# Perceiver decoder on one Trainium2 core: the block FFN computed on its chosen tokens, with rows gathered and weights addressed by register

## The chip, the cores and the metric

The program runs on one NeuronCore of a Trainium2 chip. A core has five engines with instruction queues of their own: TensorE (PE; its weight loads are listed as PEld), VectorE (DVE), ScalarE (ACT), GpSimd (POOL) and SyncE (SP), which here only issues transfers. Sixteen DMA engines move data between HBM and the on-chip memory SBUF; PE writes its results to PSUM, from where DVE or ACT copies them. The metric is the device time of one execution in microseconds (us), lower is better. All data are fp32.

## The reference

```python
x = x + L0_xattn(layernorm(x), ctx)     # 16 heads, 1024 queries in 16 sequences, 1601 keys
x = x + L0_mamba(layernorm(x))
x = x + L0_ffn(layernorm(x))            # the stage that is changed
x = x + L1_xattn(layernorm(x), ctx)     # the stage after it
x = x + L1_attn(layernorm(x))
x = x + L1_ffn(layernorm(x))

def L0_ffn(x):                          # n = 1024 tokens, IN_F 512, OUT_F 2048, 16 blocks of 128
    prob = softmax(xf @ router_w.T + router_b)
    _, idx = top_k(prob, 4)
    mask = zeros((n, 16), bool).at[arange(n)[:, None], idx].set(True)
    h = einsum('nd,ibd->nib', xf, w1b) + b1b
    h = relu(where(mask[:, :, None], h, 0))
    return einsum('nib,dib->nd', where(mask[:, :, None], h, 0), w2b) + b2
```

Each of the 1024 tokens uses 4 of the 16 blocks. Ties in the router's logits go to the lower block number.

## The kernel before

The 1024 tokens are kept as `x`, eight tiles of 128 rows by 512 (`G = 8`), normalised and transposed into `xnT` (512 features on 4 times 128 partitions, 1024 tokens along a row). The six sub-layers are stages that follow each other. A tile framework places the instructions and their semaphores; what is wrapped in `pin(...)`, or issued by `pmm`, keeps the order of the program on its engine, the rest is placed by the framework's scheduler. Every engine works its queue in order.

*The scan stage* (`st2`) ends with a loop over g = 0 to 7: `decay`, `mixing`, `gated` and `mixed` for tile g, and normalisation and transposition of tile g - 2. The last two tiles are normalised behind it, the very last one (`ln_out(G - 1, ps3)`) inside the FFN.

*The block FFN* (`st3`, L720 to L915) computes all 16 blocks for all tokens and zeroes what was not chosen. For each half q of 512 tokens, `for i in range(NBLK)` forms block i's 128 hidden units in four products of 512 columns (PE), applies bias and ReLU (ACT, L857) and multiplies by the block's mask (DVE, `masked`, L840). Then `down` forms the second product, 16 blocks into each of four row tiles, and the result is added to `x` (L900, L908).

The masks come from `route(q)` (L749 to L783): router products on PE, the rank of each logit among the 16 by comparing all pairs (four DVE passes over 1024 elements and a reduction), and `rank < 3.5`. The mask is transposed on PE, stored to HBM (`kept`, L781) and read back broadcast over all partitions, two blocks at a time (`load_mask`, L789).

Between the products of the two halves other work is placed: `fold_weights` (the next attention's query and key weights multiplied into one matrix `W`, and its bias row `wb`), `bias_part`, six pieces of the last FFN's weights that are still to be quantised (`piece_load` to `piece_turn`, with stores L187), and `ln_out` of tiles that are ready. When the second half's first products are done, the space of `w1` is released and the first context tiles for the next stage are loaded (`load_T(0)`, `load_N(0)`).

*The second cross attention* (`st4`) needs, for each tile of 128 queries, the projected queries `qtT` (`folded_q`, 512 tokens at a time), scores against 1601 keys of two sequences (`scores4`), a maximum (DVE, L965), exponentials (ACT), transposes (`transpose4`), the weighted sum (`attend4`) and an output product (`output4`). Its loop over g issues `scores4(g + 1)` ahead of the work of tile g. The context is loaded one or two tiles ahead on SP's queue.

The other stages are not touched.

Of the kernel before, what the change touches and what calls it, by code (L numbers as in the profile page):

```python
# [9 lines left out]
F32 = mybir.dt.float32  # L10
AF = mybir.ActivationFunctionType
ALU = mybir.AluOpType
# [3 lines left out]
P = 128  # L16
# [17 lines left out]
QMAX = 32767.0  # L34

# [12 lines left out]
def perceiver_kernel(ctx: ExitStack, tc: tile.TileContext, x_d, ctxT_d, ctx_d, cols_d, rows_d,  # L48
# [9 lines left out]
    def mm(out, lhsT, rhs, start=True, stop=True):  # L58
        pe.matmul(out, lhsT=lhsT, rhs=rhs, start=start, stop=stop)  # L59

# [79 lines left out]
    def add_rows(bias, g0=0, g1=G):  # L140

        for g in range(g0, g1):
# [8 lines left out]
              for n, shape in (("wgt", [D, FI]), ("wut", [D, FI]), ("wdt", [FI, D]))]  # L151
    pieces = ([(wgate_d[f * P:(f + 1) * P, :], turned[0][:, f * P:(f + 1) * P])
# [41 lines left out]
    with ExitStack() as st1:  # L194
# [19 lines left out]
        pin = tc.keep_in_program_order  # L214

        def pmm(out, lhsT, rhs, start=True, stop=True):
            pin(pe.matmul(out, lhsT=lhsT, rhs=rhs, start=start, stop=stop))  # L217

# [312 lines left out]

    with ExitStack() as st2:
# [142 lines left out]
        for g in range(G):  # L675
            if g == 4:
                make_bc(1)
            pd = decay(g)
            if g == 1:
                new = mixing(g, pd)  # L680
            if g:
                gated(g - 1, mt)
            if g >= 2:
                ln_scale(g - 2, g - 1, pin)
                xn = ln_norm(g - 2)
            mt = new if g == 1 else mixing(g, pd)
            if g:
                mixed(g - 1)
            if g >= 2:
                ln_transpose(g - 2, xn, ps2)  # L690
# [3 lines left out]
        ln_scale(G - 2, G - 1)  # L694
        ln_out(G - 2, ps2)
        ln_scale(G - 1, G)

    cT, cN, ctxt, ctxn = {}, {}, {}, {}

    def load_T(g):  # L700

        for b in (2 * g, 2 * g + 1) if g < G else ():
            cT[b] = ctxt[g % 2].tile([P, 2, LK], F32, name="cT", tag="cT")
            pin(nc.sync.dma_start(out=cT[b], in_=ctxT_d[b].rearrange("(c p) k -> p c k", p=P)))

    def load_N(g):

        for b in (2 * g, 2 * g + 1) if g < G else ():
            cN[b] = ctxn[g % 2].tile([P, KC, CD], F32, name="cN", tag="cN")
# [4 lines left out]

    with ExitStack() as st3:
# [3 lines left out]
        w2, hT = [], []  # L721
        for i in range(4):
            w2.append(big.tile([P, 4, D], F32, name="w2", tag=f"w2{i}"))
            hT.append(big.tile([P, 4, 512], F32, name="hT", tag=f"hT{i}"))
            nc.sync.dma_start(out=w2[i], in_=w2_d[:, 4 * i * D:4 * (i + 1) * D].rearrange(
                "p (i e) -> p i e", i=4))
        wq1 = load_w("wq1", wq1_d).rearrange("p (c e) -> p c e", c=4)
        wkv1 = load_w("wkv1", wkv1_d)


        bias = const.tile([P, 3], F32, name="bias", tag="bias")
        sums = const.tile([P, G + 1], F32, name="sums", tag="sums")
        wb = row(R_BV0)

        kept = dram.tile([NBLK, NT], F32, name="kept", tag="kept")
        st3a = st3.enter_context(ExitStack())
        mkp = pool(st3a, "mkp", bufs=3)
        masks = {}
        tmp = pool(st3a, "tmp3", bufs=2)
        psr = pool(st3, "psr", bufs=2, space=PSUM)  # L740
        ps3 = pool(st3, "ps3", bufs=6, space=PSUM)
        prep = pool(st3a, "prep", bufs=2)
        todo = list(range(NPREP, 3 * FC))

        lg = tmp.tile([P, G, NBLK], F32, name="lg", tag="lg", bufs=1)
        def route(q):  # L749


            pr = psr.tile([P, 512], F32, name="pr", tag="pr")
            for c in range(4):
                mm(pr[32 * c:32 * c + 32, :], rwz[:, c, :], xnT[:, c, q * 512:(q + 1) * 512])
            lp = tmp.tile([P, 512], F32, name="lp", tag="xn")
            s.copy(lp, pr)
            yield
            pr = psr.tile([P, 4, NBLK], F32, name="pl", tag="pr")
            for k in range(4):
                mm(pr[:, k, :], lp[:, k * P:(k + 1) * P], four[:, :NBLK])  # L760
            v.tensor_tensor(lg[:, 4 * q:4 * q + 4, :], pr,
                            row(R_RB, NBLK).unsqueeze(1).to_broadcast([P, 4, NBLK]), ALU.add)
            l4 = lg[:, 4 * q:4 * q + 4, :]
            shape = [P, 4, NBLK, NBLK]
            li = l4.unsqueeze(3).to_broadcast(shape)
            lj = l4.unsqueeze(2).to_broadcast(shape)
            gt = tmp.tile(shape, F32, name="gt", tag="gt", bufs=1)
            eq = tmp.tile(shape, F32, name="eq", tag="eq", bufs=1)
            v.tensor_tensor(gt, lj, li, ALU.is_gt)
            v.tensor_tensor(eq, lj, li, ALU.is_equal)  # L770
            v.tensor_tensor(eq, eq, before.unsqueeze(1).to_broadcast(shape), ALU.mult)
            v.tensor_tensor(gt, gt, eq, ALU.add)
            rank = tmp.tile([P, 4, NBLK], F32, name="rank", tag="rank", bufs=1)
            v.tensor_reduce(rank, gt, AX.X, ALU.add)
            v.tensor_scalar(rank, rank, TOPK - 0.5, None, ALU.is_lt)
            pr = psr.tile([NBLK, 4, P], F32, name="pt", tag="pr")
            for i in range(4):
                pe.transpose(pr[:, i, :], rank[:, i, :], ident)
            keepT = tmp.tile([NBLK, 512], F32, name="keepT", tag="keepT", bufs=1)
            s.copy(keepT, pr.rearrange("p a b -> p (a b)"))  # L780
            nc.sync.dma_start(out=kept[:, q * 512:(q + 1) * 512],  # L781
                              in_=keepT)
            yield  # L783

        def load_mask(n):
            q, i = divmod(n, NBLK)
            if q < 2:
                masks[n] = mkp.tile([P, 2, 512], F32, name="mk", tag="mk")
                nc.sync.dma_start(  # L789
                    out=masks[n],  # L790
                    in_=kept[i:i + 2, q * 512:(q + 1) * 512].partition_broadcast(P))

        wkT = wkv1[:, 0:1024].rearrange("p (c e) -> p c e", c=4)
        wv1 = wkv1[:, 1024:2048].rearrange("p (c e) -> p c e", c=2)
        W = wq1[:, :, 0:CD]

        def fold_weights():


            wqT = [tmp.tile([P, 2, D], F32, name="wqT", tag=n, bufs=1) for n in ("gt", "eq")]  # L800
# [4 lines left out]
            for e in range(4):  # L805
                ps = ps3.tile([P, 4, P], F32, name="ps", tag="mm")
                for c in range(4):
                    pe.transpose(ps[:, c, :], wq1[:, c, e * P:(e + 1) * P], ident)
                evac(part(e), ps.rearrange("p c d -> p (c d)"))
            ps = ps3.tile([P, D], F32, name="ps", tag="mm")  # L810
            for e in range(4):
                mm(ps, col(C_BK1 + e).to_broadcast([P, P]), part(e), e == 0, e == 3)
            s.copy(wb, ps)
            v.tensor_reduce(sums[:, G:], wb, AX.X, ALU.add)
            for h in range(2):
                ps = ps3.tile([P, 2, CD], F32, name="ps", tag="mm")
                for i in range(2):
                    c = 2 * h + i
                    for e in range(4):
                        mm(ps[:, i, :], part(e)[:, c * P:(c + 1) * P], wkT[:, e, :],  # L820
                           e == 0, e == 3)
                evac(W[:, 2 * h:2 * h + 2, :], ps)

        def bias_part(i):
            if i == 0:
                pbs.append(ps3.tile([P, 3], F32, name="pb", tag="mm"))
            for e in range(4):
                mm(pbs[0][:, i:i + 1],
                   wkT[:, e, i * P:(i + 1) * P] if i < 2
                   else col(C_BK1 + e).to_broadcast([P, P]), col(C_BQ1 + e), e == 0, e == 3)  # L830
            if i == 2:
                v.tensor_copy(bias, pbs[0])

        pbs = []
        routes = [route(q) for q in range(2)]
        next(routes[0])

        def masked(q, i):
            h = hT[i // 4][:, i % 4, :]
            v.tensor_tensor(h, h, masks[16 * q + i - i % 2][:, i % 2, :], ALU.mult)  # L840
            if i % 2:
                load_mask(16 * q + i + 5)

        def bias_product(g, pin=free):

            xw = lnp.tile([P, D], F32, name="xw", tag="xn")
            gp.tensor_tensor(xw, x[:, g, :], wb, ALU.mult)
            pin(v.tensor_reduce(sums[:, g:g + 1], xw, AX.X, ALU.add))

        for q in range(2):  # L850
            t = slice(q * 512, (q + 1) * 512)
            for i in range(NBLK):
                ps = ps3.tile([P, 512], F32, name="ps", tag="mm")
# [554 lines left out]
```

## Time and profile before

| what | value |
|---|---|
| median of 3 runs | 1940.64 us (1936.29 to 1941.37) |
| the profiled execution | 1943.53 us; its span, first to last instruction, 1941.8 us |
| mean granted clock of PE | 0.987 of full speed |
| PE, start of the FFN's first product | 1214.8 us after the span's start |
| PE, start of the second cross attention | 1456.7 us |
| PE, start of the third layer (L1 self attention) | 1600.2 us |
| tile loop of the attention, one tile of queries | 15.2 us (weighted sums start at 1486.05, 1501.21, 1516.37) |
| moved to and from HBM | 127.02 MB read, 11.60 MB written |

How to read the profile: a row of a group gives line, engine, operation, the program's names of result and operands, shapes and count, then the busy time in us, the mean of one in ns, and the idle time of the engine just before with what ended it. A matmul in fp32 appears as two passes. The ends of matmuls are modelled, so single matmuls overlap a little; the distance between starts is their pace. Times in a timeline are us from the start of the span.

### The profile page before, as it was taken

What the parts mean: (1) busy time and instruction counts of PE and PEld (TensorE: products, weight loads), DVE (VectorE), ACT (ScalarE), POOL (GpSimd) and SP (SyncE); (2) the same over time, 40 slices, a digit from 0 to 9 for tenths busy, and PEclk for the clock granted to TensorE, in tenths of its full rate; (3) what the DMA queues carried; (4) which work ended last, traced back from release to release, by engine and by line L of the source; (5) the groups of instructions that cost most, each with busy time, mean ns of one, the idle gap of its engine ahead of it and who ended that gap; (6) DMA issues with size and microseconds to landing.
All of it is one profiled execution on the core that took longest, in us unless ns stands there. A gap on an engine that the chain in (4) does not pass through costs nothing.

```text
span 1941.8 us, 41193 instructions
## 1 busy us (share of the span) xinstructions
PE 1885.0 (97%) x18111; PEld 1056.6 (54%) x18111; DVE 1047.0 (54%) x1622; ACT 790.9 (41%) x1521; POOL 651.7 (34%) x589
## 2 busy tenths in 40 slices
PE   8999999999999999999999899999999999999599
PEld 4566666666666666666666554445444554444244
DVE  4566666666666666666666455622103335229641
ACT  3355455455555554555555356201103232226700
POOL 0365556555555565554555332111002000000200
PEclk9999999999999999999999999999999999999899
DMA  6012021201120121112020211620256971010001
GB/s 220 1 47 58 12 57 47 56 14 51 53 55 15 47 57 23 47 46 58 14 56 7 88 78 34 207 55 12 80 199 261 409 284 51 0 49 17 0 0 44
DMA packets 110084, 141.28 MB, mean 73 GB/s; under 512 B 79520, under 2 KB 82096, under 8 KB 106320
## 3 DMA queue, kind: packets, MB, share of 16 engines
q1 hardware_dynamic: 109904, 138.64, 21.7%
q8 instruction: 142, 2.33, 0.5%
q14 instruction: 38, 0.31, 0.1%
HBM read 127.02 MB, written 11.60 MB: 71 GB/s over the span
## 4 chain that ended last, share of the span: by engine, by line
PE 93%; DVE 3%; issue 2%; ACT 1%; DMA 1%; POOL 0%; SPq 0%; ACTq 0%; POOLq 0%; DVEq 0%
PE ps L217 42%; PE ps L59 24%; PE sc L217 10%; PE av L217 6%; PE po L59 4%; PE u L217 2%; PE ps L133 1%; PE pbc L59 1%; DVE sc L268 1%; PE pd L59 1%; POOL gate L1285 0%; PE busy L217 0%; PE pg L59 0%; ACT at L988 0%; DVE st L116 0%
## 5 line engine op out<-in xcount | busy, mean ns | idle before, releaser
L217 PE MATMUL ps<-wkv,ctxT 128*128 128x256 f32 (+1 forms) x1664 | 412.7, 383 | 0.0
L217 PE MATMUL ps<-ctxT,wkv 128*128 128x400 f32 (+1 forms) x1024 | 408.1, 521 | 0.8 <-DMA ctxT<-in_ctxT_dram 0.8
L217 PEld LDWEIGHTS ps<-wkv,ctxT 128*128 128x128 f32 (+1 forms) x1664 | 304.0, 186 | 116.3 <-ACT kt L233 5.6
L268 DVE TENSOR_REDUCE sc<-sc 128x4 f32<-128x1664 f32 x128 | 243.0, 1898 | 197.6 <-PE sc L217 197.6
L304 POOL TENSOR_TENSOR acc<-acc,st 128x512 f32<-128x512 f32 x252 | 320.5, 1272 | 19.8
L295 DVE STREAM_TRANSPOSE st<-et 128x832 f32<-128x832 f32 x256 | 264.9, 1035 | 57.8 <-ACT et L286 51.7
L233 ACT ACTIVATE kt<-ps,cols 128x400 f32<-128x400 f32 (+1 forms) x256 | 155.1, 606 | 323.9 <-PE ps L217 323.9
L286 ACT ACTIVATE et<-sc,nm 128x416 f32<-128x416 f32 x512 | 269.6, 610 | 33.4 <-DVE nm L280 33.3
L217 PEld LDWEIGHTS ps<-ctxT,wkv 128*128 128x128 f32 x1024 | 174.5, 190 | 162.8 <-issue 81.9
L251 ACT COPY vt<-ps 128x256 f32<-128x256 f32 (+1 forms) x288 | 107.2, 372 | 180.2 <-PE ps L217 177.1
L302 POOL TENSOR_TENSOR acc<-st 128x512 f32<-128x512 f32 x63 | 80.2, 1273 | 199.3 <-DVE st L295 141.3
L217 PE MATMUL sc<-kt,xnT 32*32 32x416 f32 x4096 | 126.8, 523 | 3.6 <-ACT et L286 2.8
L59 PE MATMUL ps<-xnT,w 128*128 128x512 f32 x256 | 112.7, 594 | 0.0
L217 PE MATMUL av<-st,vt 128*32 128x64 f32 x6656 | 106.9, 220 | 3.7 <-issue 2.8
L59 PE MATMUL ps<-w,hT 128*128 128x512 f32 x256 | 110.2, 592 | 0.0
L217 PEld LDWEIGHTS av<-st,vt 128*32 128x32 f32 x6656 | 96.3, 110 | 25.4 <-issue 24.3
L175 POOL TENSOR_TENSOR w<-w,winv 128x512 f32<-128x512 f32 x36 | 37.7, 1049 | 194.1 <-DVE winv L171 192.3
L1285 POOL TENSOR_TENSOR gate<-up,gate 128x1024 f32<-128x1024 f32 x5 | 11.8, 2358 | 250.3 <-ACT up L1284 250.3
L180 POOL TENSOR_TENSOR w<-w,wsc 128x512 f32<-128x512 f32 x36 | 38.5, 1070 | 137.1 <-DVE w L179 137.1
L59 PE MATMUL ps<-xnT,wuT 128*128 128x512 f32 x192 | 82.8, 592 | 0.0
L59 PEld LDWEIGHTS ps<-w,hT 128*128 128x128 f32 x256 | 48.6, 190 | 61.2 <-issue 61.2
L59 PEld LDWEIGHTS ps<-xnT,w 128*128 128x128 f32 x256 | 47.6, 190 | 56.3 <-issue 56.2
(248 smaller groups left out, 2092.9 us busy)
## 6 DMA issues: line engine op xcount, KB each, us to landing
cT<-in_ctxT_dram SPq DMA_DIRECT2D x16, 1601.0 KB, 9.7
cN<-in_ctx_dram SPq DMA_DIRECT2D x16, 1536.0 KB, 11.1
ctxT<-in_ctxT_dram SPq DMA_DIRECT2D x15, 1601.0 KB, 6.5
mk<-kept SPq DMA_DIRECT2D x16, 512.0 KB, 4.1
w<-in_w_dram SPq DMA_DIRECT2D x1, 4096.0 KB, 13.5
w<-in_w_dram SPq DMA_DIRECT2D x4, 1024.0 KB, 6.9
w<-in_wgate_dram SPq DMA_DIRECT2D x12, 256.0 KB, 4.3
wgt<-room SPq DMA_DIRECT2D x48, 64.0 KB, 2.5
```

The source lines that it names most:

```text
L59: pe.matmul(out, lhsT=lhsT, rhs=rhs, start=start, stop=stop)
L133: pin(pe.transpose(ps[:, c, :], xn[:, c * P:(c + 1) * P], ident))
L175: pin(gp.tensor_tensor(w, w, inv.unsqueeze(2).to_broadcast([P, 16, 32]), ALU.mult))
L180: pin(gp.tensor_tensor(w, w, sc.unsqueeze(2).to_broadcast([P, 16, 32]), ALU.mult))
L217: pin(pe.matmul(out, lhsT=lhsT, rhs=rhs, start=start, stop=stop))
L233: pin(s.activation(kt[:, o:o + n], ps[:, :n], AF.Identity, bias=col(C_BK0 + c)))
L251: pin(s.copy(t[:n, :], ps[:n, :]))
L268: pin(v.tensor_reduce(top, sc[:, :, 0:KW], AX.X, ALU.max))
L286: pin(s.activation(ets[u, g][:, r, :], qks[u, g][0][:, r, 0:KW], AF.Exp, bias=nms[u, g][:, r:r + 1]))
L295: pin(v.transpose(tts[u, i][:, h, r].rearrange("p r k q -> p (r k q)"), ets[u, g][:, r, :].rearrange("p r c -> p (r c)")))
L302: pin(gp.tensor_tensor(acc, t[:, :, 0:2], t[:, :, 2:4], ALU.add))
L304: pin(gp.tensor_tensor(acc, acc, t[:, :, k:k + 2], ALU.add))
```

## The change

After the change the FFN is computed for the chosen pairs of token and block only. Each normalised tile is stored to HBM by rows (`xn_d`). The router's first half runs in the last iteration of the scan's loop, its second half behind it. From the ranks the kernel works out, for each token's four blocks, a place in a list sorted by block in which every block's part is filled up to whole tiles of 128: 47 tiles in any case. `places` counts with triangular and all-ones products on PE; one-hot tiles (written into `xnT`, which is free now) and the 32 columns `where` are multiplied on PE to give `listed`, the token number of each place. `block` holds each tile's block times 128, `btab` its bias, and `slots` the place of each token's four results.

A loop over the 47 tiles then fetches 128 rows by an indirect DMA on POOL's queue, transposes them on PE, multiplies them by their block's part of `w1` and, transposed again, of `w2`, both addressed by a register that PE loads from `block` four tiles at a time, and stores 128 rows of results to HBM (`y_d`). In the attention stage `arrive(g)` fetches four result rows for each token of tile g, again by indirect DMA, and adds them to `x`. The queries are then projected by tile (`prepare`) and not by half; the first tiles ahead of the loop, tile g + 2 inside iteration g. The masks, their store and their loads are gone. The folding of the attention's weights stands ahead of the tile loop, the six remaining weight pieces partly ahead of it and partly in it.

The diff, cut to its core:

```diff
+TILES = (NT * TOPK - P) // P + NBLK
+    xn_d = dram.tile([NT, D], F32, name="xnd", tag="xnd")
+    y_d = dram.tile([TILES * P, D], F32, name="yd", tag="yd")
...
+    def keep_rows(g, xn):
+        pin(nc.sync.dma_start(out=xn_d[g * P:(g + 1) * P, :], in_=xn))
+    def logits(q, psum, lp, lg):
+        pr = psum()
+        for c in range(4):
+            pmm(pr[32 * c:32 * c + 32, :], rwz[:, c, :], xnT[:, c, q * 512:(q + 1) * 512])
+        s.copy(lp, pr)
...
+        for k in range(4):
+            pmm(pl[:, k, :], lp[:, k * P:(k + 1) * P], four[:, :NBLK])
+        v.tensor_tensor(lg, pl, row(R_RB, NBLK).unsqueeze(1).to_broadcast([P, 4, NBLK]), ALU.add)
+    def compare(lg, gt, eq, on):
...
+        v.tensor_tensor(gt, lj, li, ALU.is_gt)
+        v.tensor_tensor(eq, lj, li, ALU.is_equal)
+        on.tensor_tensor(eq, eq, before.unsqueeze(1).to_broadcast(shape), ALU.mult)
+        on.tensor_tensor(gt, gt, eq, ALU.add)
+    def ranks(q, gt):
+        v.tensor_reduce(rk[:, t], gt, AX.X, ALU.add)
+        v.tensor_scalar(kept[:, t], rk[:, t], TOPK - 0.5, None, ALU.is_lt)
...
+        for g in range(4 * q, 4 * q + 4):
+            v.tensor_tensor(seen[:, g + 1], seen[:, g], kept[:, g], ALU.add)
+        for k in range(TOPK):
+            v.tensor_scalar(pick[:, t, k], rk[:, t], float(k), None, ALU.is_equal)
...
             pd = decay(g)
+            if g == G - 1:
...
+                for _ in logits(0, ...): pass
+                compare(lg, gt, eq, gp)
...
             if g >= 2:
+                keep_rows(g - 2, xn)
                 ln_transpose(g - 2, xn, ps2)
...
-        w2, hT = [], []
-        def route(q): ...
-        def load_mask(n): ...
-        def masked(q, i): ...
-        for q in range(2): ...
+            def places(q, on):
+                pmm(at, ahead, kept[:, 4 * q:4 * q + 4].rearrange("p g e -> p (g e)"), True, False)
+                pmm(at, ones, seen[:, 4 * q:4 * q + 4].rearrange("p g e -> p (g e)"), False, True)
...
+                for n in range(16 * q, 16 * q + 16):
+                    g, k = divmod(n, TOPK)
+                    on(n).tensor_scalar(xnT[:, k, g * P:(g + 1) * P], iota, lane[:, n:n + 1],
+                                        None, ALU.is_equal)
...
+            compare(lg, gt, eq, v)
+            places(0, lambda n: gp)
+            fold_bias()
+            bias_parts()
+            ranks(1, gt)
+            places(1, lambda n: gp if n % 4 == 3 else v)
...
+            for n in range(4 * G):
+                v.tensor_scalar(where[:, n, :], iota[:, :TILES], tileof[:, n:n + 1],
+                                ids[:, n // 4:n // 4 + 1], ALU.is_equal, ALU.mult)
+            fold_half(0)
+            for n in range(4 * G):
+                g, k = divmod(n, TOPK)
+                pmm(pw, xnT[:, k, g * P:(g + 1) * P], where[:, n, :], n == 0, n == 4 * G - 1)
+            pin(v.tensor_copy(listed, pw))
...
+        def gather(t):
+            pin(gp.indirect_dma_start(
+                out=rooms[:, t % 5, :], out_offset=None, in_=xn_d,
+                in_offset=bass.IndirectOffsetOnAxis(ap=listed[:, t:t + 1], axis=0)))
+        def turn_in(t):
+            for c in range(4):
+                pin(pe.transpose(ps[:, c, :], rooms[:, t % 5, c * P:(c + 1) * P], ident))
+            s.copy(rooms[:, 5 + t % 3, :], ps.rearrange("p c k -> p (c k)"))
+        def up_product(t):
+            if t % 4 == 0:
...
+                ins, vals = nc.values_load_multi_w_load_instructions(
+                    block[0:1, t:t + n], engines=[mybir.EngineType.PE], ...)
...
+            for c in range(4):
+                pmm(ps, rooms[:, 5 + t % 3, c * P:(c + 1) * P],
+                    w1[:, c, bass.ds(picks[t], P)], c == 0, c == 3)
+            v.tensor_copy(hs[t], ps)
+        def turn_h(t):
+            pin(pe.transpose(ps, hs.pop(t), ident))
+            s.activation(hTs[t], ps, AF.Relu, bias=btab[:, t:t + 1])
+        def down_product(t):
+            pmm(ps, hTs.pop(t), w2[:, bass.ds(picks.pop(t) * 4, D)])
+            v.tensor_copy(y, ps)
+            nc.sync.dma_start(out=y_d[t * P:(t + 1) * P, :], in_=y)
+        for t in range(5):
+            gather(t)
+        for t in range(TILES + 3):
+            if t < TILES:
+                turn_in(t)
+                if t + 5 < TILES:
+                    gather(t + 5)
+            if 0 <= t - 1 < TILES:
+                up_product(t - 1)
+            if 0 <= t - 2 < TILES:
+                turn_h(t - 2)
+            if t >= 3:
+                down_product(t - 3)
+            if t == 2:
+                load_T(0)
+            if t == 8:
+                load_N(0)
+            if t < G:
+                pin(gp.tensor_tensor(x[:, t, :], x[:, t, :], row(R_B2), ALU.add))
...
+        def arrive(g):
+            for k in range(TOPK):
+                n = TOPK * g + k
+                pin(gp.indirect_dma_start(
+                    out=ys[:, k, :], out_offset=None, in_=y_d,
+                    in_offset=bass.IndirectOffsetOnAxis(ap=slots[:, n:n + 1], axis=0)))
+            for k in range(TOPK):
+                pin(v.tensor_tensor(x[:, g, :], x[:, g, :], ys[:, k, :], ALU.add))
+            ln_stats(g, pin)
...
-        def folded_q(h): ...
-        def q_bk(h): ...
+        def prepare(g):
+            ln_transpose(g, ln_norm(g, pin), ps_mm, pin)
+            for c2 in range(2):
+                for c in range(4):
+                    pmm(ps, W[:, c, c2 * P:(c2 + 1) * P], xnT[:, c, t], c == 0, c == 3)
+                pin(s.activation(qtT[:, c2, t], ps, AF.Identity, bias=bias[:, c2:c2 + 1]))
+            pin(v.tensor_tensor(xw, x[:, g, :], wb, ALU.mult))
+            pin(v.tensor_reduce(sums[:, g:g + 1], xw, AX.X, ALU.add))
...
+        arrive(0)
+        ln_scale(0, 1, pin)
+        prepare(0)
+        scores4(0)
+        load_T(2)
+        arrive(1)
+        arrive(2)
+        ln_scale(1, 3, pin)
+        prepare(1)
         for g in range(G):
             if g + 1 < G:
                 scores4(g + 1)
...
+            if g == 0:
+                arrive(3)
+                arrive(4)
+            if g == 1:
+                for k in range(5, G):
+                    arrive(k)
+                ln_scale(3, G, pin)
...
             transpose4(g)
+            if g + 2 < G:
+                prepare(g + 2)
             if g:
                 output4(g - 1)
             attend4(g)
```

## Prediction

> **What bounds the kernel now.** I read the page's busy times first, then the chain of waits, then busy times by stage, then the timelines around the two ends of the block FFN, and last the transfers.
>
> The page: TensorE (PE) is the bound, and the FFN's two products are two of its costly groups.
>
> ```profile
> PE 1885.0 (97%) x18111; PEld 1056.6 (54%) x18111; DVE 1047.0 (54%) x1622; ACT 790.9 (41%) x1521; POOL 651.7 (34%) x589
> L59 PE MATMUL ps<-xnT,w 128*128 128x512 f32 x256 | 112.7, 594 | 0.0
> L59 PE MATMUL ps<-w,hT 128*128 128x512 f32 x256 | 110.2, 592 | 0.0
> ```
>
> The columns are count, busy us, mean ns, idle. 128 products stand as 256 passes, so an fp32 product of 512 columns takes two passes of 0.44 us. Together 222.9 us, which the change attacks.
>
> Busy times in three stretches (FFN, second cross attention, the rest) and in one short one near the end:
>
> ```profile
> 1215.00:1457.00 242.00, 242.00 (x654) 113.79 (x653) 63.81 (x108) 30.09 (x48) 25.38 (x21) 1.00 0.33 111
> 1457.00:1600.00 143.00, 140.52 (x900) 74.35 (x899) 47.09 (x104) 45.67 (x93) 10.80 (x13) 1.00 0.82 319
> 1600.00:1942.00 342.00, 310.14 (x755) 139.24 (x753) 163.63 (x265) 110.91 (x156) 11.79 (x5) 0.95 0.07 25
> ...
> 1846.00:1852.00 6.00, 5.37 (x8) 2.17 (x9) 5.51 (x7) 0.23 (x1) 0.58 (x1) 0.52 0.00 0
> ```
>
> After the length come PE, weight loads, DVE, ACT, POOL, granted clock, DMA share, GB/s. In the FFN PE never rests: routing, masks and folding are hidden. In the attention PE rests 2.5 us.
>
> The timeline of PE, with durations that I use below:
>
> ```profile
> 1214.35 0.60 PE L133 MATMUL ps<-ident,xn 128*128 128x128 f32 x4
> 1606.99 1.16 PE L59 MATMUL sc<-KT,QT 64*128 64x128 f32 x8
> 1846.63 5.35 PE L217 MATMUL busy<-gate,ident 128*128 128x512 f32 x6 [22.41 <-DVE gate L1291]
> 1851.93 2.74 PE L217 MATMUL busy<-wdT,ident 128*128 128x512 f32 x6
> ```
>
> Four transposes take 0.60, eight 128-column passes 1.16. Six passes after a rest of 22.41 us took 2.6 us longer than six later ones: the clock of 0.52 above.
>
> Transfers (KB each, median us from issue to landing):
>
> ```profile
> w<-in_wup_dram SPq DMA_DIRECT2D x12, 256.0 KB, 3.8
> w<-in_wgate_dram SPq DMA_DIRECT2D x12, 256.0 KB, 4.3
> out_dram<-ot SPq DMA_DIRECT2D x8, 256.0 KB, 2.0
> ```
>
> A gathered tile, 128 rows of 2 KB, has 256 KB too.
>
> **The sum's start.** The profiled execution took 1943.5 us, span 1941.8 and 1.7 around it, 2.9 above the median of 1940.6. PE starts the FFN at 1214.8, the attention at 1456.7 (241.9 later) and the third layer at 1600.2 (143.5 later). What follows is unchanged.
>
> **Step 1: the last scan iteration, +2.7.** The first half's router now stands in it. PE's passes there only move (they were in the FFN), but DVE gets 0.23 + 1.23 + 1.22 (logits, two comparisons) ahead of the product that PE waits for. POOL's two comparison passes are under PE's work.
>
> **Step 2: the list, which nothing covers.** The FFN's first product needed one transposed tile; the first gather needs the whole list. From the last output product's end, 1214.5 + 2.7 = 1217.2: add, statistics, root, reciprocal, normalisation 0.63 + 0.68 + 0.17 + 0.29 + 0.12 + 0.65 = 2.5, and in DVE's queue between them two roundings and a transpose of weight pieces (0.89 + 0.89 + 0.67): 1222.2. Transposes, copy, router passes, copy, logit passes 0.60 + 0.59 + 1.06 + 0.57 + 0.96, and 1.0 for five hand-overs (some 0.2 each): 1227.0. Logits 0.23, four comparisons 4.9, reduction 1.2, kept 0.2, four picks (0.2) and four running sums (0.15) 1.4, the first half's places 1.2: 1236.1. Then PE's small products 0.5, eight-odd DVE passes of 256 or 512 elements 2.7 (0.35 and 0.67, by 1.22 for 1024), seven small ones 1.1, twelve one-hot tiles 2.4 (0.2 each, by 0.43 for 512), 32 columns of the list 5.4 (0.17 each, by the 0.16 of the smallest rows), a reduction 0.69, the copy 0.16: list at 1249.1. One gather 4.0 (between 3.8 and 4.3): first tile at 1253.1, 38.3 after the FFN's start. The folding of the attention's weights (some 16 us of PE) fits under this wait.
>
> **Step 3: the tile loop.** 47 tiles of 128 rows always, whatever is chosen. PE per tile: four transposes 0.60, eight passes of 128 columns 1.16, one transpose 0.15, two passes of 512 0.86: 2.77. Beside it per tile DVE 0.9, ACT 0.9, POOL one issue: all covered. No row shows a product with a register address (five per tile, a register instruction ahead of each). From below 0; from above 0.35 each, what SP's queue takes to issue a transfer; I take 0.08, twice the 38 ns of a queue's semaphore instruction, its nearest kin: 3.17 per tile. Twelve register loads: 0.04 to 1.6 (the 32 KB store of the mask landed in 1.6); I take 0.4. So 149 + 5 + 4 for draining three tiles. Gathers are five tiles ahead (16 us) and land in 4.3: covered. Row stores stand in SP's queue behind context loads that land in 9.7 and 11.1, but three buffers and two PSUM banks are 16 us: covered; were the cover gone, some 5 us each. Loop's end 1411, 45.7 earlier than now.
>
> **Step 4: rows back, T = 1411.** 32 more gathers, into one set of four buffers, and DVE takes them in program order behind each score maximum. I price POOL's issue at 1.0 (its nearest row, 1.05 for a 512-column pass; bounds 0.35 from SP's issue and 2.36, its longest pass) and 3.0 more to land (2.0 to 4.3), so four gathers take 7.0. Copy 0.69, issue and store 2.3: T+3.0. Row set 0 landed T+10.0, last add and statistics T+11.6, root and normalisation T+12.8, transposes, copy, 16 passes, bias T+17.0, scores 5.5 and maximum 2.2 T+24.7. Set 1 is there: four adds and statistics 3.7, T+28.4. Set 2's issue starts when set 1's first buffer is read, T+25.4: landed T+32.4, normalised T+35.2, projected T+39.4, scores and maximum T+47.1. Set 3 T+50.8; set 4 issued T+47.8, landed T+54.8; tile 2 projected T+60.8. Behind this projection in PE's queue stands the first weighted sum: it starts at T+60.8, where it now starts 29.4 after the stage's start. Then sum and scores 11.2, maximum 2.2, set 5 T+77.9, set 6 landed T+81.9, set 7 T+86.6, tile 3 projected T+93.2; the second weighted sum starts at T+94.1, now at 44.5: +49.6. Four later tiles are projected one by one inside the loop: transposes 0.6, 16 passes 2.3, a wait for ACT's copy 0.9, four times: +15.2. Loads, masks and POOL's adds of the bias lie under it. And four rests of PE of 10 to 19 us, each followed by work at half clock: 4 x 2.6 = 10.4 by the row above (below: 0). Step 4: +75.2.
>
> The Trainium skill ("TensorE: Matmul & The Clock Gate", section "What's actually happening") states that an idle window of about 3.4 us halves the clock until some 3.4 us of work are done; the row shows it for one rest of 22 us alone, and by the rule the four rests cost about 1.7 us each, 7 in place of 10.4, so its sum would be 3.6 us lower.
>
> The same skill speaks against the gathers ("SBUF — State Buffer", section "SBUF: two separate sides"): POOL can't write descriptors while DVE holds the shared port, 620 ns becoming 3100. This trace shows such a clash only for computing (a rounding of 0.43 us took 1.25 beside a POOL pass); by the page's figure the 16 gathers of sets 2, 4, 6 and 7 would cost 2.1 us more each, an estimate of 34 us more.
>
> **Sum.** -45.7 + 75.2 = +29.5: 1973.0 from the profiled time, 1970 from the median.
>
> Bounds: with both register prices and the rests at their least and four gathers in 3.4, the loop ends 23.5 earlier and step 4 is 27 less: 1920. With 0.35 per product the loop is 78 longer: 2048. With four gathers in 12.3, step 4 is 25 more: 1995.
>
> **Rivals.**
> - *The tiles run at the array's pace and the rows come back cheaply* (faster). For it: 222.9 us of products become 47 x 2.0, and no view shows a queue that must be slow. Against it: list and first rows alone are 38 + 29 us uncovered. It decides once the unknown costs fall 29.5 us below my values; at their least 1920.
> - *Register addresses bind PE* (slower still): the sequencer works out five addresses per tile and PE starves. For it: ten short passes per tile leave it little time to run ahead, and the profile has no such row. Against it: 64 products of 13 ns spacing (0.86 us) are issued without a gap now. Price 0.27 x 5 x 47 = 63, with slower register loads 78: 2048.
> - *Both cancel*: a loop at 2.77 and sets at 7.0 with cheap rests land within 0.3%: 1940.
>
> That the change might not shrink the work is no rival: 47 tiles are fixed and 128 products of 512 columns are gone.
>
> **How the numbers follow.** Forecast 0.56, faster rival 0.25, register rival 0.15, cancelling 0.04. About 0.3% is what a measurement of this kernel tells from no change. So faster 0.25, same 0.04, slower 0.71. The likeliest case alone spans 1950 to 2005. The range 1920 to 2048 reaches to both outer rivals' prices and leaves out about half of each.
>
> **What would show it.** Step 2: PE's first transpose of a gathered tile near 1253, with PE idle before it. Step 3: tiles 3.2 us apart; idle put down to "issue" or PE's sequencer means register cost. Step 4: DVE waiting for DMA on the returned rows, and PE on DVE, until the second weighted sum near T+94; then attention iterations of 19 us where they are 15. It is wrong if DVE's adds find their rows always landed (the faster rival), or if tiles are over 4 us apart (the register one).

## The result and the profile after

The changed kernel took 2002.84 us (median of 4 runs, 1999.33 to 2007.43), the kernel before 1940.14 (4 runs, 1936.29 to 1941.37): a ratio of 1.0328 with a 95% interval of 1.0301 to 1.0355, so it is slower by 62.7 us where +29.5 was forecast. The profiled execution took 1999.33 us, 55.8 more than the profiled one of before, and what follows accounts for these 55.8.

The page's line of busy times, after:

```profile
PE 1819.9 (91%) x18466; PEld 1086.9 (54%) x18466; DVE 1116.5 (56%) x1814; ACT 819.0 (41%) x1600; POOL 735.7 (37%) x687
```

PE did 65.1 us less than before (1885.0), yet the kernel is longer: the rests grew by more than the work shrank.

Busy times by stage (length, PE, weight loads, DVE, ACT, POOL, granted clock, DMA share, GB/s): list with the first tile's transposes, tile loop, return with the attention, the rest.

```profile
1215.00:1264.00 49.00, 42.08 (x188) 31.62 (x187) 33.19 (x102) 6.41 (x13) 24.16 (x36) 0.74 0.42 149
1264.00:1387.00 123.00, 112.34 (x701) 85.22 (x701) 51.22 (x110) 43.96 (x93) 57.58 (x57) 0.96 0.77 247
1387.00:1657.00 270.00, 170.23 (x1014) 105.11 (x1014) 90.74 (x183) 57.55 (x117) 43.64 (x45) 0.79 0.56 211
1657.00:1998.00 341.00, 308.38 (x753) 138.33 (x751) 163.19 (x263) 109.91 (x154) 11.78 (x5) 0.96 0.09 33
```

The rest is as it was (341 against 342). The list and the loop end at T = 1387.3, 69.4 earlier than the FFN of before (1456.7; forecast 45.7 earlier). From T to the third layer (1656.7) the changed kernel needs 269.4 us, where before needed 143.5: +125.9, forecast +75.2. Nearly 100 us of this stage are rests of PE, and the granted clock in it is 0.79. Added up: -69.4 + 125.9 - 0.7 = +55.8. So the sign came from the right place, and its size is a matter of the attention stage.

The loop's first two tiles on PE's timeline (start, us, what; in brackets the rest ahead and what ended it), and then one full turn of the loop, after:

```profile
1259.97 0.63 PE L965 MATMUL ps<-ident,xnT 128*128 128x128 f32 x4
1263.99 0.67 PE L965 MATMUL ps<-ident,xnT 128*128 128x128 f32 x4 [3.39 <-DMA xnT<-xnd,listed]
...
1268.69 0.60 PE L965 MATMUL ps<-ident,xnT 128*128 128x128 f32 x4
1269.13 1.06 PE L67 MATMUL ph<-w,xnT 128*128 x8
1270.02 0.27 PE L988 MATMUL ph<-ident,h 128*128 128x128 f32 x1
1270.13 1.02 PE L67 MATMUL py<-w,hT 128*128 x2
1270.99 0.60 PE L965 MATMUL ps<-ident,xnT 128*128 128x128 f32 x4
```

Tiles start 2.30 us apart, not 3.17. The durations (0.60 + 1.06 + 0.27 + 1.02 = 2.95) overlap in the rows; only the distances between starts add up: 0.44 + 0.89 + 0.11 + 0.86 = 2.30.

The first tile is turned at 1260.0, as soon as PE is through with the folding (1259.9); its gather was issued at 1255.64, so it was landed within 4.3 us. PE's rest of 3.39 us is for the second tile, whose gather took 6.72 us from issue (1257.13) to landing.

The returned rows in the chain of waits (start of the issue, us to the landing), after:

```profile
1395.05 10.16 DMA ys<-yd,slots
...
1424.49 7.37 DMA ys<-yd,slots
...
1454.88 3.56 DMA ys<-yd,slots
...
1484.70 8.29 DMA ys<-yd,slots
```

The prediction gave a gather 1.0 us of issue and 3.0 to land. The three slow ones (in sets 0, 2 and 6) have context loads beside them: the DMA engines are busy throughout, with a share of 0.99 or more. The one of 3.56 us (set 4) has none, and the share around it is 0.45.

One attention iteration, before (PE's timeline), for comparison, and then after, on PE and on ACT:

```profile
1537.12 5.55 PE L217 MATMUL sc<-cT,qtT 128*64 128x512 f32 x32
1542.60 0.44 PE L1006 MATMUL ps<-ident,us 128*128 128x128 f32 x2
1542.87 1.66 PE L986 MATMUL ps<-ident,es 128*128 128x128 f32 x13
```

```profile
1540.46 5.55 PE L67 MATMUL sc<-cT,qtT 128*64 128x512 f32 x32
1545.94 0.44 PE L1133 MATMUL ps<-ident,us 128*128 128x128 f32 x2
1546.22 1.04 PE L1113 MATMUL ps<-ident,es 128*128 128x128 f32 x8
1550.61 0.94 PE L1113 MATMUL ps<-ident,es 128*128 128x128 f32 x5 [3.36 <-ACT uT L1135]
1551.59 1.11 PE L141 MATMUL ps<-ident,xn 128*128 128x128 f32 x4
1553.37 3.79 PE L67 MATMUL ps<-xnT,wq 128*128 128x128 f32 x16 [0.68 <-ACT xnT L143]
```

```profile
1548.37 1.54 ACT L1099 ACTIVATE es<-sc,sh 128x1536 f32<-128x1536 f32 x1 [15.88 <-DVE sh L1095]
...
1550.19 0.37 ACT L1135 COPY uT<-ps 128x256 f32<-128x256 f32 x1
1550.44 1.72 ACT L1115 COPY at<-ps 128x512 f32<-128x512 f32 x4
```

Before, the 13 transposes of the exponentials ran through. Now PE stops after 8: the buffers that it fills are emptied by ACT's copies, and these stand in ACT's queue behind the next tile's exponentials, which wait for the next tile's score maximum. ACT rests 15.88 us ahead of them. The diff pins this order (exponentials of g+1, then uT, then at). After the rest the projection's 16 passes take 3.79 us, where 2.3 was put for them. From the second on, the weighted sums follow each other after 26.4, 24.5, 24.2, 27.5, 21.2 and 10.8 us, where before it was 15.2 three times, 15.9 twice and 10.5.

### The profile page after: what moved, and what is told of

Read it like the earlier page. It is cut to its first block, busy times and chain, and to the rows that moved or that the text cites. A ratio compares the mean times of both kernels' runs of the same rounds, so it can differ in the third digit from the quotient of the medians.

```text
span 1997.6 us, 42893 instructions
## 1 busy us (share of the span) xinstructions
PE 1819.9 (91%) x18466; PEld 1086.9 (54%) x18466; DVE 1116.5 (56%) x1814; ACT 819.0 (41%) x1600; POOL 735.7 (37%) x687
## 4 chain that ended last, share of the span: by engine, by line
PE 83%; DVE 5%; issue 4%; DMA 4%; ACT 2%; POOL 1%; SPq 0%; POOLq 0%; DVEq 0%; ACTq 0%
PE ps L67 41%; PE ps L62 11%; PE sc L67 9%; PE av L67 6%; PE po L62 4%; PE u L67 2%; DMA ys<-yd,slots 2%; PE ph L67 2%; PE py L67 2%; PE ps L141 1%; PE ps L965 1%; DMA yd<-y 1%; PE pr L67 1%; PE pbc L62 1%; DVE sc L273 1%
## 5 line engine op out<-in xcount | busy, mean ns | idle before, releaser
L141 PE MATMUL ps<-ident,xn 128*128 128x128 f32 x192 | 32.4, 307 | 52.0 <-DVE xn L134 49.2
L62 PE MATMUL po<-wdT,gate 128*128 128x512 f32 x178 | 76.6, 592 | 0.0
L62 PE MATMUL ps<-xnT,wgT 128*128 128x512 f32 x176 | 75.7, 592 | 0.0
L1195 DVE TENSOR_REDUCE mx<-ps 128x1 f32<-128x512 f32 x48 | 33.0, 688 | 69.0 <-ACT gate L1379 65.5
```

The costliest lines, as they stand in the source:

```text
L141: pin(pe.transpose(ps[:, c, :], xn[:, c * P:(c + 1) * P], ident))
```

## The experiments

Eleven kernels ran, each four times but e6, which ran once. The kernel before, beside them, had medians between 1940.4 and 1940.7. The ratio stands to the kernel before, with its 95% interval; times are set against the 2002.8 of the changed kernel, whose four runs spread over 8 us (interval 1.0301 to 1.0355). Differences of 3 to 5 us are within that, and for them the traces say more than the medians.

**e1: ScalarE's order.** `scores4` is cut in two, and its exponentials are written behind the next projection:

```diff
             if g + 2 < G:
                 prepare(g + 2)
+            if g + 1 < G:
+                exps4(g + 1)
```

> ScalarE's order alone is changed: the two exponentials of tile g+1 are written after tile g's copies and the projection of tile g+2, no longer ahead of uT. Theory (the pinned order makes PE wait 3.4 to 4.7 us per iteration for uT and lets its clock fall): iterations of 19 us instead of 24 to 27, PE's wait for uT under 0.5 us, time 2002.8 - 32 = 1971 us. Rival (the added projections on a slow clock set the iteration, the wait only takes up their time): iterations stay above 22 us, time not under 1990.

1976.97 us, ratio 1.0191 (1.0172 to 1.0210): 25.9 faster. PE's timeline of e1, the same iteration:

```profile
1536.01 5.55 PE L67 MATMUL sc<-cT,qtT 128*64 128x512 f32 x32
1541.50 0.44 PE L1138 MATMUL ps<-ident,us 128*128 128x128 f32 x2
1541.77 1.66 PE L1118 MATMUL ps<-ident,es 128*128 128x128 f32 x13
1544.43 0.63 PE L141 MATMUL ps<-ident,xn 128*128 128x128 f32 x4 [1.00 <-DVE xn L134]
1545.73 2.05 PE L67 MATMUL ps<-xnT,wq 128*128 128x128 f32 x16 [0.67 <-ACT xnT L143]
```

The 13 transposes run through as before, no wait for uT is left in the four iterations with a projection, and here the projection takes 2.05 us instead of 3.79 with not one pass fewer: the rest had also cost the clock. Two of the four iterations are like this and take 19.1 us, the term of the prediction; in the other two the projection still takes 3.68 and 3.38 us, and they take 20.7 and 22.9. From the second weighted sum to the third layer it is 123.0 us, 25.3 less than the 148.3 of the changed kernel; the whole gain is there, 6 us short of the theory's.

**e2: context loads of the second pair behind set 0.**

```diff
-        load_T(1)
-        load_N(1)
...
         ln_scale(0, 1, pin)
+        pin(nc.sync.dma_start(out=kept_d, in_=rstd[:, 0:1]))
+        load_T(1)
         prepare(0)
         scores4(0)
         load_T(2)
+        load_N(1)
```

> Context loads of the second pair alone are moved: cT(1) goes behind a 512-byte store that needs set 0's statistics, cN(1) behind cT(2). Theory (6.4 MB of context loads lengthen the landing of the returned rows): set 0's last gather lands 3 to 5 us after its issue instead of 10.2, its last add ends at T+12 instead of T+18, the first weighted sum starts 6 to 10 us nearer to T than T+78.7, time about 1995. Rival (the gather is slow by itself): landing stays at 8 to 10 us and the time at 2003.

1998.33 us, ratio 1.0295 (1.0278 to 1.0312): 4.5 lower by the medians, not clear of the scatter. In the chain of waits of e2 the set-0 row corresponds to the 10.16 above:

```profile
1400.07 3.77 DMA ys<-yd,slots
```

So the gather itself needs what the prediction gave it (1.0 + 3.0), and 6.4 us of the 10.2 came of the second pair's context loads beside it. Set 0's statistics begin 12.1 us after the loop's end instead of about 18.7. Most of the gain is lost again: set 1's adds still stand behind the first score maximum, and the sets after that meet the same loads, now later (9.28 us in set 2). The first weighted sum starts at T+75.9 instead of T+78.7, the third layer at T+266.6 instead of T+269.4. (T itself is 5.2 us later in this trace, since the list was ready later; the edit does not touch it.)

**e3: two sets of buffers.**

```diff
+        yss = ys, xnT[:, :, 512:1024]
         def arrive(g):
+            ys = yss[g % 2]
```

> The returned rows alternate between two sets of four buffers (the second in the columns of xnT that tiles 4 to 7 use later). Theory (one set of buffers makes each set's gathers wait for the adds of the set before): set 1's gathers are issued right behind set 0's, set 2's right after set 0's adds, first weighted sum at about T+62 instead of T+78.7 and second at about T+97 instead of T+121, time about 1977. Rival (DVE's order behind the score maxima and the landing set the pace): first sum not earlier than T+72, time not under 1993.

1989.03 us, ratio 1.0249 (1.0226 to 1.0272): 13.8 faster, between the theory's 26 and the rival's 10. First sum T+70.3, second T+108.5. The gathers did move up, but DVE adds sets 1 and 2 behind the first maximum, and at the second tile the row of e3 is

```profile
1488.78 1.33 PE L1115 MATMUL ps<-ident,es 128*128 128x128 f32 x5 [16.88 <-ACT uT L1137]
```

and on ACT's timeline of e3 stands just ahead of it

```profile
1488.17 0.30 ACT L128 ACTIVATE rstd<-mv,eps 128x5 f32<-128x5 f32 x1 [11.90 <-DVE mv L125]
```

ACT's queue holds one root (the square root of the normalisation) for sets 3 to 7 ahead of uT: PE waits for set 7's rows in order to go on with the first tiles. In the changed kernel the same rest stands at this place and is 21.33 us, the longest of the stage. It is the wait of e1 again, here for DMA.

**e4: context loads of the first pair in pieces.** `load_T(0)` and `load_N(0)` become fourteen loads, one every second tile, pinned between the row stores.

> In the tile loop the context loads of the first pair (6.3 MB) go out in fourteen pieces of at most 0.8 MB, one every second tile from tile 6 on, in order with the row stores. Theory (row stores and the first gathers queue behind 1.5 MB loads): the first gather lands in 4 to 5 us instead of 8, PE's stall of 7.9 us near 1298 and most of that near 1321 go, the loop ends 12 to 15 us earlier (T about 1373), time about 1989. Rival (volume binds: DMA share 0.87 in these stretches): the stalls are spread over more tiles, T moves by under 4 us.

1998.84 us, ratio 1.0302 (1.0285 to 1.0319): 4.0 lower by the medians, not clear of the scatter. What PE waited for in the loop (us in total, times, longest), after and then e4:

```profile
PE py L67 <- DVE y L996: 7.6, 1, 7.6
PE ps L965 <- DMA xnT<-xnd,listed: 4.1, 2, 3.4
PE ph L988 <- DVE h L984: 1.9, 1, 1.9
```

```profile
PE ph L988 <- DVE h L984: 10.5, 7, 3.2
PE ps L965 <- DMA xnT<-xnd,listed: 2.0, 1, 2.0
```

The long stall went and seven smaller ones took its place; from the first tile to T it is 123.8 us instead of 127.4, and T moved by 2.3. That is the rival's figure; that the volume is the reason is not shown by it. The longest of the new ones (3.18 before 1312.1) has DVE resting 4.24 us for the store of a weight piece, ahead of the copies of h and y.

**e5: fixed weight addresses.**

```diff
-                    w1[:, c, bass.ds(picks[t], P)], c == 0, c == 3)
+                    w1[:, c, (t % 16) * P:(t % 16 + 1) * P], c == 0, c == 3)
...
-            pmm(ps, hTs.pop(t), w2[:, bass.ds(picks.pop(t) * 4, D)])
+            pmm(ps, hTs.pop(t), w2[:, (t % 16) * D:(t % 16 + 1) * D])
```

> The products of tile t take the weights of block t mod 16 at fixed addresses, so the choice of the weights by block is left out; the register loads stay. Theory (a product with a register address costs PE nothing that shows): tiles stay 2.30 us apart, the loop ends as before, time 2003 within 4. Rival (0.08 us per product, as the prediction took, hidden in the 2.30): tiles 1.9 us apart, the loop 19 us shorter, time 1984.

1999.50 us, ratio 1.0303 (1.0284 to 1.0321): 3.3 lower by the medians, within the scatter. Tiles of e5 start 2.30 us apart (1268.49, 1270.79, 1273.09), as with registers. A product whose weights are addressed by a register costs PE nothing that shows.

**e6: the first half's comparison on DVE.** `compare(lg, gt, eq, gp)` becomes `compare(lg, gt, eq, v)`.

> The first half's two comparison passes go from POOL (2.4 us each) to DVE (1.22 each). Theory (POOL's passes slow the DVE passes beside them): DVE's second masking product takes 1.2 us instead of 3.37, the normalisation 0.55 instead of 1.08, the last output product of the scan ends within 0.5 us of where it did, since DVE now has 2.4 us more to do. Rival (the 3.37 has another cause): it stays above 2.5 us.

One run, 1999.4 us, which tells no difference in time. The second masking product on DVE, after and then e6:

```profile
1205.77 3.37 DVE L687 TENSOR_TENSOR mt<-mt,ea 128x1024 f32<-128x1024 f32 x1
```

```profile
1207.32 1.22 DVE L687 TENSOR_TENSOR mt<-mt,ea 128x1024 f32<-128x1024 f32 x1
```

Normalisation 0.54 instead of 1.08. POOL's passes at L568 and L569 were not free: DVE lost 2.7 us beside them. The scan's last output product ended 3.3 us earlier (1214.7 against 1218.0), where a shift of at most 0.5 was expected: it began 1.6 earlier, and its passes took 3.67 us instead of 5.37. The list came only 0.7 us earlier: its last normalisation ran beside a weight piece on POOL (1.30 us where 0.55 was measured without), and the router's passes began 1.0 us earlier only.

**e7: e1 to e4 together.**

> The four edits of e1 to e4 together. If they act on different stretches their gains add: 2002.8 - 25.9 - 4.5 - 13.8 - 4.0 = 1955. Rival (the same waits are counted twice, first of all the wait of the second tile's transposes for uT): 1965 to 1975.

1957.13 us, ratio 1.0091 (1.0072 to 1.0110). The four gains add up to 48.2, measured together 45.7, so they act on different stretches in the main.

**e8: another order of the row return,** on top of e7. `arrive` is cut into `fetch` and `add`:

```diff
+        fetch(0)
+        fetch(1)
+        add(0)
...
         for g in range(G):
             if g + 1 < G:
                 scores4(g + 1)
+            if g + 2 < G:
+                add(g + 2)
+                rows4(g + 2)
+            if g + 1 < G:
+                maxima4(g + 1)
```

`add` has the four additions, the statistics, the next free set's gathers and a root of its own; `rows4` has the normalisation and the folded sums.

> As e7, and the order of the row return is changed: sets 0 and 1 are gathered at once, set g+2 is added and normalised on DVE ahead of the score maximum of tile g+1 and has its own root on ScalarE, no set waits at the second tile for sets 5 to 7. Theory (order and buffers, not the transfers, make the return expensive): first weighted sum at T+42, every iteration 16 to 20 us, third layer at T+184, time about 1910, under the kernel before. Rival (the transfers of the rows set the pace): first sum later than T+60 and iterations above 22 us, time not under 1945.

1919.90 us, ratio 0.9887 (0.9866 to 0.9908): 37.2 less than e7, and below the kernel before by 20.5 us. First weighted sum at T+47.4 (before: 29.4 after the stage's start), iterations of 18.3, 20.8, 20.2, 21.0, 20.4, 15.9 and 10.5 us, third layer at T+189. The theory asked for a little more (T+42, T+184, 1910), the rival's figures are far off: order and buffers made the return expensive. The edit changes several places of the order at once, and what each is worth was not tried. Its page:

```profile
PE 1808.5 (94%) x18466; PEld 1075.6 (56%) x18466; DVE 1122.0 (58%) x1819; ACT 829.2 (43%) x1611; POOL 737.5 (38%) x687
```

The same instructions of PE as in the changed kernel (18466), and 83 us less. Transfers begin to show: PE waits for cT in three iterations, 4.0 us in all, and the DMA share between 1426 and 1574 is 0.82.

**e9: no rest ahead of the first tile,** on top of e8: 14 idle products between the loop and `prepare(0)`.

> On top of e8: 14 idle products of 512 columns keep PE busy between the last down product and the first tile's transposes. Theory (a rest of 14 us halves the clock for the work behind it, 2.6 us each time as the prediction took): the first tile's transposes, projection and scores take 0.66 + 2.05 + 5.55 us instead of 1.09 + 3.78 + 6.22, 2.8 us less; but the second tile waits for its rows until 1412.8, so the time falls by under 1 us, 1919. Rival (the passes are slow because the context loads run beside them): they stay at 1.09, 3.78 and 6.22.

1920.85 us, ratio 0.9897 (0.9880 to 0.9914): no gain: PE waits 4.76 us for set 1's normalised tile, in e8 2.38. The transposes (0.66) and the scores (5.60) came as the theory had them, the projection (3.63) did not. What that shows of the clock is in the last section.

**e10: weight pieces late,** on top of e8: loaded at tile 16 + 4n, scaled at 22 + 4n, turned at 24 + 4n, and all DVE work of the loop pinned.

> On top of e8: the six weight pieces are prepared from tile 16 on, each loaded six tiles ahead, in a fixed order with the copies of the loop on DVE. Theory (the loop's rests come from copies of h that stand in DVE's queue behind weight pieces waiting for their load or for POOL, 10.5 us in e4): from the first gathered tile's transposes to T 112 us (47 x 2.30 + 4) instead of 121, time about 1911. Rival (the transfers of rows and contexts bind the loop): still 118 or more.

1919.14 us, ratio 0.9892 (0.9874 to 0.9910). From the first tile to T it is 120.9 us (e8: 123.6), as the rival had it. Most of the rests moved behind tile 16, where DVE's queue stands 4.62, 3.22 and 5.32 us at copies of y that wait for row stores. PE's rests in the loop are 13.6 us in the changed kernel, 12.5 in e4 and 9.1 here, and behind the long ones stands a store or a load; that the volume of transfers sets them (DMA share 0.77 in the changed kernel's loop) is likely, but no run took volume away.

**e11: the pins alone.** `pin(...)` is taken off the two exponentials and the copies of at and uT.

> The changed kernel with the pins taken off four ScalarE operations of the attention loop alone: two exponentials, the copies of at, the copy of uT. Theory (the pins cause the waits for uT, not the order of the row return): the copies go ahead of the next exponentials again, iterations of 19 to 21 us, time 1975 to 1982 as in e1. Rival (e1 gained through the place behind the projection): waits for uT of 3 us or more stay, time not under 1992.

1985.17 us, ratio 1.0230 (1.0210 to 1.0250): 17.7 faster than the changed kernel. PE's transposes run through again and no wait for uT is left in the four iterations with a projection, which take 23.7, 21.4, 19.9 and 26.4 us. The theory's mechanism holds, its figures were too low (time by 3 us, and only one iteration in its 19 to 21): now the exponentials stand ahead of xnT, and PE waits 1.5 to 2.9 us for that. So taking off the pins gives 17.7 of e1's 25.9 us; that the other 8.2 are the better place is a difference of two runs, not a test of its own.

## Why the prediction was wrong, and where it was right

- *Step 1 (+2.7).* Measured +3.5: the last output product ended at 1218.0. "POOL's two comparison passes are under PE's work" was wrong in its reason: they slowed DVE (e6), and PE waited for DVE.
- *Step 2 (list at 1249.1, first tile at 1253.1).* Measured 1255.3 and 1260.0. The 32 columns took 7.65 us instead of 5.4, and the list's 64 passes on PE ended 2.8 us behind them. The first gather was priced rightly (at most 4.3 us where 4.0 was put), and PE did not stand idle before it, as the sign said, but folded weights. It rested before the second tile: that gather took 6.7 us, 5.5 without the context loads beside it (e4) and at most 3.9 without the weight pieces' transfers as well (e10, where PE no longer waits for it).
- *Step 3 (3.17 per tile).* Wrong on both its terms, in the same direction. "2.77" added durations where distances count (2.30), and "I take 0.08" for a register address is 0 (e5): 47 x 0.87 = 41 us too much. "Row stores ... three buffers and two PSUM banks are 16 us: covered" failed too: DVE's copy of y waited 6.58 us for a store and PE stood 7.64 us. It came back at other places when that was mended (e4, e10). In all the loop took 127.4 us from its first tile instead of 158.
- *Step 4 (+75.2).* This is the step that failed; it measured +125.9. Three of its terms:
  - "3.0 more to land" is the gather alone (3.77 with the issue in e2). The context loads at the start of the stage were costed at nothing: with the next pair's 6.3 MB on the same DMA engines it was 10.16 (e2 against the changed kernel). Set 0's statistics ended at T+19.6 instead of T+11.6, and the first weighted sum came at T+78.7 instead of T+60.8. Moving these loads alone does not bring it back (T+75.9 in e2), since the next sets then meet them; the order of e8 does (T+47.4).
  - The second one came at T+121 instead of T+94.1. The order that the prediction walked through on DVE (set, maximum, set) was right, and two buffer sets alone gave 13.8 (e3). What it missed is that ACT is walked through in program order too: uT behind the root of sets 3 to 7 (21.33 us of rest at the second tile).
  - "Four later tiles are projected one by one ...: +15.2". Iterations of 24 to 27.5 us instead of 19 are 34 us in all (148.3 - 114.2 from the second sum on). The pins on ACT were in the diff and were costed at nothing; with the order changed (e1) 25.3 of these 34 us go, and with the pins alone taken off (e11) the whole kernel is 17.7 us faster.
- *The rests (+10.4).* The size per rest fits (in the first tile 1.09 against e1's 0.63, 3.79 against 2.05 and 6.06 against 5.55: 2.7 us), but there were more than four: all eight projections took 3.6 to 3.8 us. A rest of 10 us is not needed for it (last section).
- *The rivals.* Register addresses don't bind PE (e5). The faster rival asked for the tiles "at the array's pace", which came, and for rows that "come back cheaply", which did not; e8 makes them cheap with the same PE instructions, and takes 1919.9 us where that rival was worked out at 1920 (by other terms, so the closeness is chance). Of the estimate of 34 us more from the page on the two sides of SBUF nothing was seen: POOL's 32 issues of returned rows took 0.94 to 1.30 us each.

In short, the size of the result is the difference of two errors: the loop was 30.6 us better than forecast, the list and first gather 6.9 worse, the return and the attention 50.7 worse; 6.9 - 30.6 + 50.7, less 0.7 in the rest, is the 26.3 us by which the profiled execution exceeds the forecast.

## What to carry to other kernels

When a change pins an engine's order, walk that queue once with the work's due times as carefully as PE's own: an early operation that waits for the next tile holds every copy behind it, and here it cost 18 to 26 us. Add up a pipelined engine's work from distances between starts, never from durations, or short passes look a quarter dearer than they are (2.95 us for 2.30 here). And ask of each new transfer what else is on the DMA engines at that moment: the same gather took 3.8 and 10.2 us.

## What the runs showed of the hardware

**The clock falls after less than one long rest.** In e9 PE was busy without a gap until 1401.8, rested 2.27 us, did four transposes in 0.66, and rested 0.68. Its timeline and the windows around (length, PE, weight loads, DVE, ACT, POOL, clock, DMA share, GB/s):

```profile
1404.04 0.66 PE L141 MATMUL ps<-ident,xn 128*128 128x128 f32 x4 [2.27 <-DVE xn L134]
1405.37 3.63 PE L67 MATMUL ps<-xnT,wq 128*128 128x128 f32 x16 [0.68 <-ACT xnT L143]
1408.92 5.60 PE L67 MATMUL sc<-cT,qtT 128*64 128x512 f32 x32
```

```profile
1404.00:1405.30 1.30, 0.66 (x4) 0.42 (x4) 1.26 (x3) 0.57 (x1) 1.00 (x2) 1.00 0.85 215
1405.30:1407.00 1.70, 1.63 (x7) 1.63 (x8) 1.59 (x5) 0.02 (x1) 1.09 (x3) 0.50 2.43 151
```

(The DMA column is not used here: in windows as short as these it can exceed 1.) The transposes still ran at clock 1.00 and the projection behind them at 0.50, 3.63 us instead of the 2.05 of a warm one. No single rest was longer than 2.27 us. In e1 still less was enough, and not every time: in each of the four iterations with a projection PE does 15 transposes (some 2 us), rests 1.0, does four transposes (0.63), rests 0.68, and then projects. The four projections took 3.68, 2.05, 2.05 and 3.38 us; the granted clock was 0.50 in the first and 1.00 in the third.

The Trainium skill ("TensorE: Matmul & The Clock Gate", section "What's actually happening") puts the throttle down to an idle window of about 3.4 us, which runs freely. That the same sequence is slow twice and fast twice agrees with a window that runs freely. Its length agrees only if the transposes count for little or nothing: from the start of the first rest to the projection it is 3.6 us in e9 but 2.3 in e1, and there only the stretch from the end of the scores, all transposes included, is longer than the window (4.2). No run tells transposes from other short work.

**DVE beside POOL.** A DVE product of two operands from SBUF, 1024 columns, took 3.37 us with POOL's two-operand passes beside it and 1.22 without (e6). It began 0.1 us behind a POOL pass of 2.41 us and ended 1.1 behind that pass's end; a product beside the POOL pass before, with one operand in PSUM, took 1.21. The Trainium skill ("SBUF — State Buffer", section "SBUF: two separate sides") states that two such operations on operands in SBUF share a pair of ports as an exclusive lock, which the rows bear out.

**A fine point of gathers.** POOL issues one of 128 rows of 2 KB every 1.25 us (0.94 and a gap of 0.30). With no transfers but gathers on the DMA engines the fourth of a set is landed 3.77 us after its issue began, so four take 7.5 us (e2); the prediction's 7.0 was near.
